# One recurrence step: the state kept once with four query products, the filtered attention turned for 6 and 10 sequences, the context's channels picked by products

## The chip, the cores and the metric

The kernel runs on one core of one Trainium2 chip. Its time is the device time of one execution in microseconds, and the number that counts is the median of several runs. The profile is one further execution, recorded with its instructions.

The engines are named as in the profile: PE is TensorE (PEld its loads of stationary operands, PE its matmuls), DVE is VectorE, ACT is ScalarE, POOL is GpSimd, SP is SyncE, which issues most DMAs here.

## The reference

The whole computation is two decoder layers for 16 sequences of 128 positions and 1024 channels. Layer 0 has a bidirectional state-space mixer, a cross-attention and a quantized feed-forward. Layer 1 has grouped-query attention, a recurrent attention decoder and a binarized feed-forward. A layer norm follows each. The change lies in the recurrent decoder of layer 1, which walks through the 128 positions one after the other:

```python
def step(carry, tgt):
    s, c, alpha = carry
    f = lax.conv_general_dilated(alpha, conv_w, (1,), 'SAME', dimension_numbers=('NCH', 'OIH', 'NCH'))
    e = jnp.einsum('a,bta->bt', va, jnp.tanh(enc_proj + (s @ Wa_s.T)[:, None, :] + jnp.einsum('bft,af->bta', f, Wa_f) + ba))
    e = jnp.where(mask, e, jnp.float32(-1e+30))
    alpha_new = jax.nn.softmax(e, axis=1)[:, None, :]
    g = jnp.einsum('bt,btd->bd', alpha_new[:, 0], hbatch)
    y = jnp.tanh(g @ L_gy_w.T + L_gy_b + s @ L_sy.T) @ L_yy_w.T + L_yy_b
    rec = tgt @ L_ys.T + s @ L_ss.T + g @ L_gs_w.T + L_gs_b
    ig, fg, cg, og = jnp.split(rec, 4, axis=1)
    c_next = _sig(fg) * c + _sig(ig) * jnp.tanh(cg)
    s_next = _sig(og) * jnp.tanh(c_next)
    return ((s_next, c_next, alpha_new), y)
```

Here s and c have 128 channels for each of the 16 sequences, alpha is the attention over the 128 positions of the memory, hbatch (the memory) has 256 channels, the filter has 10 channels of width 101, and rec has four gates of 128 channels. A position needs s, c and alpha of the position before it. The products with tgt and the outputs y do not sit inside the loop of the kernel: it keeps s and g of every position, and makes y from them afterwards.

## The kernel before

The stages follow each other: the mixer, the cross-attention, the feed-forward, the grouped-query attention, the recurrence (`decoder_scan`), and a last stage that makes the decoder's outputs and the final feed-forward (`stage_last`). While the attention's last group runs, `decoder_prepare` loads and prepares the constants of the recurrence on SP's queue (the products with tgt, scaled weights, filter bands). Everything is fp32 except where F32R or BF16 is named.

`decoder_scan` is a Python loop over the 128 positions, fully unrolled. `K.ordered` takes the order in which the loop issues its instructions and fixes it on PE, DVE, ACT, POOL and SP. So each engine runs its instructions in the order of the code, and waits come only from data and from buffers (PSUM tags such as `s1` and `s2` have one buffer each).

A position's step goes like this:

1. The PSUM tile `pf`, four banks of 512 columns (16 sequences of 32 memory positions in each), holds the argument of the tanh: the memory's projection, which ACT copies in (`pf<-enc`, L1128 and L1132), and on top of it, by products that accumulate (`onto`, L1056), the filtered attention (`waf` with `R`) and the state's query (`swr` with the 0/1 matrix `slot`).
2. `energies` (L1068, L1072): ACT takes the tanh of four sequences at a time into `th`, and PE multiplies it with `va`, which gives the energies.
3. Maximum, exponential, a transpose (L1122, L1152), and `aD`, in which each sequence's attention is a column of its own. The products of `aD` with the memory `hb` (L1149) give the context `pg`: 128 rows and 256 channels, where only row 32 * (b % 4) + b holds sequence b.
4. Sums and their reciprocals, and `gn`, the context divided by them (L1160, DVE). PE has meanwhile filtered the attention by products with banded matrices (L1164), and ACT scales the result into `fs` (L1169).
5. `gn` is turned so that channels lie on partitions: two transposes of 128 channels (L1175), each followed by a copy on DVE (L1176) that picks the 16 rows that hold sequences and writes them twice, for 32 columns of `gT`. POOL copies each half into the history (`ghist`, L1178).
6. The gates `gq`: own terms (L1081), the state's part (L1125: four column groups of 32, `sT` stationary) and the context's part (L1185: two halves of the channels times four groups). Then a tanh (L1188), two DVE operations to the new cell state (L1191, L1195), and the tanh `tc` of it (L1197).
7. `fs` is transposed into `ff` (L1199), and DVE turns the filtered attention of 8 sequences into `R` (L1201). A bf16 product that nobody reads (`keep_awake`) follows on PE, and the `waf` products for these 8 sequences (L1056).
8. The state `s` (L1206) is written four times side by side, 128 columns, and DVE transposes it in blocks of 32 (L1209): `sT` then holds the state four times, on 128 columns.
9. At the top of the next step, POOL copies the state into its history (L1092). One product with `sT` stationary gives the query `psw` on all 128 rows (L1099). DVE turns `R` for the other 8 sequences (L1100), splits the query into two F32R parts (`hi` L1102, `swr` L1104), and PE adds the `waf` products of the other 8 sequences and then the four `slot` products (L1056). With these, `pf` is complete and the next tanh can start.

Of the kernel before, what the change touches and what calls it, by code (L numbers as in the profile page):

```python
# [15 lines left out]
ALU = mybir.AluOpType  # L16
# [7 lines left out]
P = 128  # L24
NB = 16
# [880 lines left out]
LA_K = 101  # L906
LA_CHN = 10
LA_CH = 8


def decoder_prepare(K, keep, one, work, bank, pre, band, src):
# [5 lines left out]
    nc, a = K.nc, K.a  # L917
    D = {}
# [3 lines left out]
    D["gs"] = K.t(keep, [P, 2, 512], "gs")  # L922
    nc.sync.dma_start(D["gs"], a["la_gsT"].rearrange("(k p) n -> p k n", p=P))
    D["va"] = K.t(keep, [P, 63], "vaE")
    for n, k in (("ss", "la_ssT"), ("Was", "la_WasT"), ("waf", "la_Waf4"), ("dup", "k_dup")):
        D[n] = K.t(keep, [P, a[k].shape[1]], n)
        nc.sync.dma_start(D[n], a[k])

# [5 lines left out]
    for s in range(4):  # L934
        n = min(3, LA_CHN - 3 * s)
# [74 lines left out]
def decoder_scan(K, D, pre, ghist, shist, piece):  # L1010
# [5 lines left out]
    nc = K.nc  # L1016
    with ExitStack() as st:
        own = K.pool(st, "d_own")
        work = K.pool(st, "d_work", 2)
        ps = K.pool(st, "d_ps", 1, PSUM)  # L1020
# [4 lines left out]
        for k in range(4):  # L1025
            nc.tensor.matmul(pf[:, k].rearrange("p b t -> p (b t)"), zr[32 * k:32 * k + 32, :], D["slot"][32 * k:32 * k + 32, :],
                             start=True, stop=True, skip_group_check=True)
# [7 lines left out]
        aDb = bass.AP(aD.tensor, aD.offset, [aD.ap[0], [33, NB]])  # L1035
        pb = [K.t(own, [P, LA_CH, P], f"pb{i}") for i in range(2)]
        for t in pb:
# [1 line left out]

        z = K.t(work, [P, 5, 32], "z")  # L1040
        nc.vector.memset(z[:, 4], 0.0)
        sT = K.t(work, [P, P], "sT", bufs=4)
        nc.vector.memset(sT, 0.0)
        ff = K.t(ps, [P, 512], "ff")
        nc.vector.memset(ff, 1.0)

        taken = [bass.AP(ff.tensor, ff.offset + 8 * h, [ff.ap[0], [1, 8], [0, 2], [32, 16]]) for h in range(2)]
        def load_pre(ch):
            for q in range(4):
                nc.sync.dma_start(pb[ch % 2][32 * q:32 * q + 16, :, :],  # L1050
                                  pre[:, ch * LA_CH:(ch + 1) * LA_CH, q * P:(q + 1) * P])

        def onto(lhs, rhs, first, n):

            for k in range(4):
                nc.tensor.matmul(pf[:, k, first:first + n].rearrange("p b t -> p (b t)"), lhs[32 * k:32 * k + 32, :],  # L1056
                                 rhs[32 * k:32 * k + 32, 32 * first:32 * (first + n)], start=False, stop=True, skip_group_check=True)

        def keep_awake(n):

            for _ in range(n):
                idle = K.t(ps, [P, 512], "s2")
                nc.tensor.matmul(idle, D["identb"], D["wake"], start=True, stop=True)
# [16 lines left out]
        def own_terms(gq, l):  # L1080
            nc.tensor.matmul(gq, D["dup"], pb[(l // LA_CH) % 2][:, l % LA_CH, :], start=True, stop=False, skip_group_check=True)  # L1081

# [3 lines left out]
        R = None  # L1086
        traced = nc.cur_bb.bb.instructions
        for l in range(P):
            last = l + 1 == P
            if l % LA_CH == 0 and l + LA_CH < P:  # L1090
                load_pre(l // LA_CH + 1)
            nc.gpsimd.tensor_copy(shist[:, :, l], sT[:, 0:16])  # L1092
# [3 lines left out]
            if l:  # L1096

                psw = K.t(ps, [P, P], "s1")
                nc.tensor.matmul(psw, sT, D["Was"], start=True, stop=True)  # L1099
                nc.vector.transpose(R[:, 256:512].rearrange("p (b c) -> p b c", c=32), taken[1])  # L1100
                hi = K.t(work, [P, P], "hi", F32R)
                nc.vector.tensor_copy(hi, psw)  # L1102
                swr = K.t(work, [P, P], "swr", F32R)
                nc.vector.scalar_tensor_tensor(swr, hi.bitcast(F32), D["lohi"], psw, ALU.mult, ALU.add)  # L1104
                onto(D["waf"], R, 8, 8)
                onto(swr, D["slot"], 0, NB)

            pe = [K.t(ps, [P, P], "s1"), ff[:, 0:P]]
# [3 lines left out]
            gq = K.t(ps, [P, P], "gq")  # L1112
# [9 lines left out]
            nc.tensor.transpose(pT[0], ex[0], K.ident)  # L1122
            if l and not last:
                for q in range(4):
                    nc.tensor.matmul(gq[32 * q:32 * q + 32, :], sT[:, 0:32], D["ss"][:, q * P:(q + 1) * P], start=False, stop=False,  # L1125
                                     skip_group_check=True)
            if not last:
                nc.scalar.copy(pf[:, 0], D["enc"][:, 0])  # L1128
# [18 lines left out]
            for g in range(4):  # L1147
                for i in range(4):
                    nc.tensor.matmul(pg[32 * i:32 * i + 32, :], aD[:, 4 * g + i, :], D["hb"][:, 4 * g + i, :],  # L1149
                                     start=(g == 0), stop=(g == 3), skip_group_check=True)  # L1150
# [8 lines left out]
            gn = K.t(work, [P, 2, P], "gn")  # L1159
# [9 lines left out]
                nc.scalar.activation(fs.rearrange("p c t -> p (c t)"), ff[:, 0:3 * P], AF.Copy, scale=rx)  # L1169
                K.tc.add_manual_dep(traced[-1], copied.name, SYNC, reason="copies")  # L1170

            gT = K.t(work, [P, 2, 2, 16], "gT", bufs=4)
            for c in range(2):
                pgT = K.t(ps, [P, P], ("s2", "s1")[c])
                nc.tensor.transpose(pgT, gn[:, c], K.ident)  # L1175
                nc.vector.tensor_copy(gT[:, c].rearrange("p e (g i) -> p e g i", i=4),  # L1176
                                      bass.AP(pgT.tensor, pgT.offset, [pgT.ap[0], [0, 2], [4, 4], [33, 4]]))
                nc.gpsimd.tensor_copy(ghist[:, c, :, l], gT[:, c, 0, :])  # L1178
            if last:
                break  # L1180
            if l == 0:
                own_terms(gq, l)
            for c in range(2):
                for q in range(4):
                    nc.tensor.matmul(gq[32 * q:32 * q + 32, :], gT[:, c].rearrange("p e b -> p (e b)"),  # L1185
                                     D["gs"][:, c, q * P:(q + 1) * P], start=False, stop=(c == 1), skip_group_check=True)

            nc.scalar.activation(z[:, 0:4].rearrange("p g u -> p (g u)"), gq, AF.Tanh)  # L1188
# [4 lines left out]
            now, z = z, K.t(work, [P, 5, 32], "z")  # L1193
            C = z[:, 4]
            nc.vector.scalar_tensor_tensor(C, AB[:, 1], 0.5, AB[:, 0], ALU.mult, ALU.add)  # L1195
            tc = K.t(work, [P, 32], "tc")
            nc.scalar.activation(tc, C, AF.Tanh, scale=0.5)  # L1197
            for c in range(3):
                nc.tensor.transpose(ff[:, c * P:(c + 1) * P], fs[:, c, :], K.ident)  # L1199
            R = K.t(work, [P, 512], "R", bufs=1)  # L1200
            nc.vector.transpose(R[:, 0:256].rearrange("p (b c) -> p b c", c=32), taken[0])  # L1201
            keep_awake(1)
            onto(D["waf"], R, 0, 8)

            s = K.t(work, [P, 4, 32], "s")
            nc.vector.scalar_tensor_tensor(s, now[:, 2].unsqueeze(1).to_broadcast([P, 4, 32]), 1.0,  # L1206
                                           tc.unsqueeze(1).to_broadcast([P, 4, 32]), ALU.add, ALU.mult)
            sT = K.t(work, [P, P], "sT", bufs=4)
            nc.vector.transpose(sT, s.rearrange("p j u -> p (j u)"))  # L1209
        order()  # L1210


def stage_decoder(K, D, pre, src, out):
    with ExitStack() as st:
        hist = K.pool(st, "d_hist")
        ghist = K.t(hist, [P, 2, NB, P], "ghist")
        shist = K.t(hist, [P, NB, P], "shist")
        mkeep = K.pool(st, "m_keep")
        with ExitStack() as s2:
            W, piece = last_weights(K, mkeep, K.pool(s2, "m_raw"))  # L1220
            decoder_scan(K, D, pre, ghist, shist, piece)
        D["room"].close()
        stage_last(K, W, ghist, shist, src, out)
# [234 lines left out]
def rope_constants():  # L1458

    f = np.float32  # L1460
    theta, factor, hi, lo, L0 = 500000.0, 32.0, 4.0, 1.0, 2048
    idx = np.arange(0, 32, 2, dtype=f) / f(32)
    freq = f(1.0 / (2.0 * np.pi)) * np.power(f(theta), -idx)
    scaled = np.where(freq < f(lo / L0), freq / f(factor), freq)
    smooth = np.clip((f(L0) * freq - f(lo)) / f(hi - lo), f(0), f(1))
    mid = (f(1) - smooth) * (freq / f(factor)) + smooth * freq
    freq = np.where((freq >= f(lo / L0)) & (freq <= f(hi / L0)), mid, scaled).astype(f)
    phase = f(2.0 * np.pi) * np.arange(P, dtype=f)[:, None] * freq[None, :]
    emb = np.concatenate([phase, phase], -1)

    sign = np.where(np.arange(32) % 32 < 16, -1.0, 1.0).astype(f)
    return [np.ascontiguousarray(np.tile(t.astype(f).T, (4, 1))) for t in (np.cos(emb), np.sin(emb) * sign)]


def shape_constants():
    f = np.float32
    o = {}
    r = np.arange(P)

    step, seq = r // 8, r % 8  # L1480
    same = seq[:, None] == seq[None, :]
    o["k_seq_masks"] = np.stack([same & (step[:, None] < step[None, :]), same & (step[:, None] > step[None, :])], 1).astype(f)
    o["k_step_masks"] = np.stack([step[:, None] < np.arange(16)[None, :], step[:, None] > np.arange(16)[None, :]], 1).astype(f)
    o["k_cos"], o["k_sin"] = rope_constants()
    o["k_causal"] = np.where(r[:, None] >= r[None, :], 0.0, -1e30).astype(f)

    o["k_slot"] = (r[:, None] % 16 == np.arange(512)[None, :] // 32).astype(f)

    o["k_half"] = np.stack([1.0 - (r % 32 // 8 == 1), (r % 32 // 8 == 1)], 1).astype(f)
    o["k_lohi"] = np.where(r % 32 < 16, 0.0, -1.0).astype(f).reshape(P, 1)  # L1490

    n = np.arange(64)
    n = np.arange(16)

    o["k_dup"] = (r[:, None] == (r - r % 32 + r % 16)[None, :]).astype(f)

    o["k_quad"] = (r[:, None] % 32 == np.arange(8)[None, :]).astype(f)
    o["k_time"] = np.tile(np.arange(P, dtype=f), (P, 1))
    return o


def layout(i):
# [61 lines left out]
    o["mo_gT"] = c(i[p + "gate_w"].T)  # L1564
    o["mo_b"], o["mo_in"], o["mo_out"] = (c(i[p + n]) for n in ("bias", "in_channel_scale", "out_channel_scale"))
    o.update(shape_constants())
    return o

# [13 lines left out]
```

## Time and profile before

| what | value |
|---|---|
| median of 3 runs | 3615.65 us (3613.06 to 3617.14) |
| profiled execution, its own time | 3607.57 us |
| span of the profiled execution | 3605.8 us |
| granted PE clock, mean over the span | 0.948 |
| recurrence | from about 1890 us to about 3290 us |
| one step, gn to gn | 10.96 us |
| PE / DVE / ACT / POOL busy | 88% / 51% / 38% / 27% |

A row of the profile names the line, the engine, the operation, what it writes and reads, the shape, and the count. For PE, `128*32` means a tile of 128 rows and 32 columns of the array. Each record of a matmul is one pass: fp32 products have two records each, transposes one. The ends of matmuls are modelled, so two groups on PE can seem to overlap a little. PSUM tiles of the same tag share a name, so `s` in these rows stands for `psw`, `pgT`, `pg` and `pe`.

### The profile page before, as it was taken

The page shows a single profiled execution, that of the slowest core. Times are in us where ns is not written, and L with a number is a line of the kernel's source. Part 1 is how long each engine was busy: PE and PEld are TensorE (multiplying, and loading weights), DVE is VectorE, ACT ScalarE, POOL GpSimd, SP SyncE. Part 2 cuts the span into 40 slices and gives each one's busy share as a digit, 9 for nine tenths or more (in the row PEclk, how much of TensorE's full clock was granted, in tenths as well). Part 3 has the DMA queues.
Part 4 walks back from the last instruction along what each step waited for, and adds up shares of the span by engine and source line. Part 5 has one row for each costly group of instructions (what it writes and reads, how often), then busy time and mean ns, then how long its engine had stood idle before and what let it go on. Part 6 is the DMA issues. An engine that isn't in the chain of part 4 may idle for free.

```text
span 3605.8 us, 60750 instructions
## 1 busy us (share of the span) xinstructions
PE 3168.9 (88%) x24202; PEld 1696.6 (47%) x24202; DVE 1852.8 (51%) x5044; ACT 1378.1 (38%) x3521; POOL 978.3 (27%) x1106
## 2 busy tenths in 40 slices
PE   7778886888899999999998888888888888887998
PEld 3444453666454555455544444444444444443455
DVE  5785775666244545453334444444444444444665
ACT  4433332111032333232225555555555555553211
POOL 3334763455233233331110111111111111112453
PEclk8778998999989999998999999999999999998898
DMA  5001222111410101022211000000000000001111
GB/s 184 1 1 47 98 78 93 47 59 47 148 36 12 47 24 47 24 81 69 87 40 41 5 11 11 5 11 5 10 5 10 5 10 5 5 2 48 35 59 47
DMA packets 72213, 144.12 MB, mean 40 GB/s; under 512 B 10042, under 2 KB 34490, under 8 KB 71930
## 3 DMA queue, kind: packets, MB, share of 16 engines
q1 hardware_dynamic: 65562, 122.74, 10.3%
q10 hardware_dynamic: 6368, 17.50, 1.2%
q8 instruction: 191, 3.13, 0.4%
q14 instruction: 92, 0.75, 0.1%
HBM read 102.47 MB, written 39.06 MB: 39 GB/s over the span
## 4 chain that ended last, share of the span: by engine, by line
PE 53%; DVE 9%; ACT 9%; issue 2%; POOL 1%; DMA 0%; POOLq 0%; DVEq 0%; ACTq 0%; SPq 0%
PE p L784 8%; ACT th L1068 7%; PE s L1149 7%; PE p L855 6%; PE pf L1056 4%; PE p L1002 3%; PE m L1386 3%; PE gq L1185 2%; PE ff L1164 2%; PE t L833 2%; PE s L812 2%; PE p L797 2%; PE ff L1072 2%; PE s L1099 2%; DVE R L1201 1%
## 5 line engine op out<-in xcount | busy, mean ns | idle before, releaser
L1068 ACT ACTIVATE th<-pf 128x512 f32<-128x512 f32 x512 | 264.4, 602 | 331.1 <-PE pf L1056 331.0
L1178 POOL COPY ghist<-gT 128x16 f32<-128x16 f32 x256 | 44.8, 214 | 979.5 <-DVE gT L1176 979.5
L821 ACT ACTIVATE s<-s,nm 128x128 f32<-128x128 f32 x512 | 198.2, 389 | 253.1 <-DVE nm L818 220.4
L1149 PE MATMUL s<-hb,aD 128*32 128x256 f32 x4096 | 275.5, 387 | 0.6 <-DVE aD L1138 0.6
L1056 PE MATMUL pf<-R,waf 32*128 32x256 f32 x2032 | 181.4, 426 | 69.6 <-DVE R L1201 69.6
L855 PE MATMUL p<-ga_Wo,cT 128*128 128x512 f32 x512 | 228.7, 595 | 0.0
L1132 ACT COPY pf<-enc 128x512 f32<-128x512 f32 x381 | 224.8, 590 | 8.1
L784 PE MATMUL p<-xT,ga_Wq 128*128 128x512 f32 x512 | 226.4, 597 | 0.0
L824 POOL TENSOR_TENSOR s<-s,rs 128x512 f32<-128x512 f32 x128 | 133.3, 1041 | 321.6 <-DVE rs L823 314.8
L1077 DVE TENSOR_REDUCE nm<-s 128x1 f32<-128x128 f32 x128 | 37.4, 292 | 288.2 <-PE s L1072 288.2
L91 POOL TENSOR_TENSOR ln_rs<-ln_ve,neghalf 128x1 f32<-128x1 f32 x96 | 55.6, 582 | 380.8 <-DVE ln_ve L89 363.9
L784 PEld LDWEIGHTS p<-xT,ga_Wq 128*128 128x128 f32 x512 | 95.4, 190 | 113.8 <-issue 111.0
L855 PEld LDWEIGHTS p<-ga_Wo,cT 128*128 128x128 f32 x512 | 93.8, 190 | 113.8 <-issue 111.7
L1149 PEld LDWEIGHTS s<-hb,aD 128*32 128x32 f32 x4096 | 106.5, 109 | 84.2 <-DVE aD L1138 46.1
L1056 PEld LDWEIGHTS pf<-R,waf 32*128 32x128 f32 x2032 | 79.3, 182 | 134.1 <-DVE R L1201 118.8
L1072 PE MATMUL s<-th,vaE 128*32 128x128 f32 x2048 | 109.3, 286 | 36.4 <-ACT th L1068 28.5
L1169 ACT ACTIVATE fs<-ff,rx 128x384 f32<-128x384 f32 x127 | 73.8, 581 | 172.4 <-DVE rx L1167 169.1
L835 DVE COPY pT<-t 128x512 f32<-128x512 f32 x128 | 88.0, 687 | 87.6 <-PE t L833 87.3
L1072 PE MATMUL ff<-th,vaE 128*32 128x128 f32 x2048 | 109.3, 286 | 16.2
L1002 PE MATMUL p<-xT,qT 128*128 128x512 f32 x256 | 115.2, 603 | 0.0
L856 DVE TENSOR_TENSOR xr<-p,xr 128x512 f32<-128x512 f32 x32 | 22.1, 692 | 168.5 <-PE p L855 168.5
L812 PE MATMUL s<-kT,qT 32*128 32x128 f32 x1024 | 108.0, 315 | 0.0
(342 smaller groups left out, 6878.4 us busy)
## 6 DMA issues: line engine op xcount, KB each, us to landing
x<-x SPq DMA_DIRECT2D x95, 512.0 KB
xt<-xT SPq DMA_DIRECT2D x8, 1024.0 KB
x<-x ACTq DMA_DIRECT2D x16, 512.0 KB
xr<-x SPq DMA_DIRECT2D x16, 512.0 KB
x<-xr SPq DMA_DIRECT2D x16, 512.0 KB
out<-x ACTq DMA_DIRECT2D x16, 512.0 KB
ga_Wq<-ga_Wq SPq DMA_DIRECT2D x2, 2048.0 KB
ga_Wo<-ga_Wo SPq DMA_DIRECT2D x2, 2048.0 KB
```

The costliest lines, as they stand in the source:

```text
L784: nc.tensor.matmul(pq, lhsT, xT[:, k].rearrange("p i t -> p (i t)"), start=(k == 0), stop=(k == 7))
L812: nc.tensor.matmul(psc[n][:, r, :], qT[sl, 4 * kc + r, i, :], kT[sl, kc, i, :], start=True, stop=True)
L821: nc.scalar.activation(s[:, r, :], s[:, r, :], AF.Exp, bias=nm[:, r:r + 1], accum_out=sm[:, r:r + 1])
L824: nc.gpsimd.tensor_tensor(s, s, rs.unsqueeze(2).to_broadcast([P, 4, P]), ALU.mult)
L855: nc.tensor.matmul(po, cT[:, k, :], w["o"][h][:, k, :], start=(k == 0), stop=(k == 7))
L1002: nc.tensor.matmul(py, xT[:, k, b % 4, :], ys[:, k, :], start=(k == 0), stop=(k == 7))
L1056: nc.tensor.matmul(pf[:, k, first:first + n].rearrange("p b t -> p (b t)"), lhs[32 * k:32 * k + 32, :], rhs[32 * k:32 * k + 32, 32 * first ...
L1068: nc.scalar.activation(th.rearrange("p i (k t) -> p i k t", t=32), pf[:, :, 4 * g:4 * g + 4, :].rearrange("p k i t -> p i k t"), AF.Tanh)
L1072: nc.tensor.matmul(pe[32 * i:32 * i + 32, :], D["va"][:, 31 - b:63 - b], th[:, i, :], start=False, stop=(g % 2 == 1), skip_group_check=True)
L1132: nc.scalar.copy(pf[:, k], D["enc"][:, k])
L1149: nc.tensor.matmul(pg[32 * i:32 * i + 32, :], aD[:, 4 * g + i, :], D["hb"][:, 4 * g + i, :], start=(g == 0), stop=(g == 3), skip_group_che ...
L1386: nc.tensor.matmul(pm[:, h, :], xp[:, k, :], w[:, k, h * 512:(h + 1) * 512], start=(k + n == 0), stop=(k + n == 8))
```

## The change

The change has three parts, all in the recurrence.

The context's channels: the two transposes and the two copies are replaced. A new constant `pick` (128 rows, 32 columns, 0 or 1) has a one in column j at row 32 * (b % 4) + b with b = j % 16. Each half of `gn` is now the stationary operand of an fp32 product with `pick`, which puts the picked 16 sequences, twice, straight into 32 columns of one PSUM tile. One copy of 64 columns moves both halves to `gT`, and one POOL copy writes the history. `decoder_prepare` loads `pick` with one DMA more.

The state: `s` and `sT` have 32 columns instead of 128. The query is made by four products, each of which writes 32 rows of `psw` with the same 32 columns of `sT` stationary.

The filtered attention: `R` is turned for 6 sequences first and for 10 in the next step, where it was 8 and 8, and the `waf` products are split alike.

```diff
+LA_ONE = 6
 ...
-    for n, k in (("ss", "la_ssT"), ("Was", "la_WasT"), ("waf", "la_Waf4"), ("dup", "k_dup")):
+    for n, k in (("ss", "la_ssT"), ("Was", "la_WasT"), ("waf", "la_Waf4"), ("dup", "k_dup"),
+                 ("pick", "k_pick")):
         D[n] = K.t(keep, [P, a[k].shape[1]], n)
         nc.sync.dma_start(D[n], a[k])
 ...
-        sT = K.t(work, [P, P], "sT", bufs=4)
+        sT = K.t(work, [P, 32], "sT", bufs=4)
         nc.vector.memset(sT, 0.0)
 ...
-        taken = [bass.AP(ff.tensor, ff.offset + 8 * h, [ff.ap[0], [1, 8], [0, 2], [32, 16]]) for h in range(2)]
+        taken = [bass.AP(ff.tensor, ff.offset + first, [ff.ap[0], [1, n], [0, 2], [32, 16]])
+                 for first, n in ((0, LA_ONE), (LA_ONE, NB - LA_ONE))]
 ...
                 psw = K.t(ps, [P, P], "s1")
-                nc.tensor.matmul(psw, sT, D["Was"], start=True, stop=True)
-                nc.vector.transpose(R[:, 256:512].rearrange("p (b c) -> p b c", c=32), taken[1])
+                for k in range(4):
+                    nc.tensor.matmul(psw[32 * k:32 * k + 32, :], sT, D["Was"], start=True, stop=True)
+                nc.vector.transpose(R[:, 32 * LA_ONE:].rearrange("p (b c) -> p b c", c=32), taken[1])
 ...
-                onto(D["waf"], R, 8, 8)
+                onto(D["waf"], R, LA_ONE, NB - LA_ONE)
                 onto(swr, D["slot"], 0, NB)
 ...
-            gT = K.t(work, [P, 2, 2, 16], "gT", bufs=4)
+            pgT = K.t(ps, [P, 2, 32], "s2")
             for c in range(2):
-                pgT = K.t(ps, [P, P], ("s2", "s1")[c])
-                nc.tensor.transpose(pgT, gn[:, c], K.ident)
-                nc.vector.tensor_copy(gT[:, c].rearrange("p e (g i) -> p e g i", i=4),
-                                      bass.AP(pgT.tensor, pgT.offset, [pgT.ap[0], [0, 2], [4, 4], [33, 4]]))
-                nc.gpsimd.tensor_copy(ghist[:, c, :, l], gT[:, c, 0, :])
+                nc.tensor.matmul(pgT[:, c], gn[:, c], D["pick"], start=True, stop=True)
+            gT = K.t(work, [P, 2, 32], "gT", bufs=4)
+            nc.vector.tensor_copy(gT, pgT)
+            nc.gpsimd.tensor_copy(ghist[:, :, :, l], gT[:, :, 0:16])
 ...
             R = K.t(work, [P, 512], "R", bufs=1)
-            nc.vector.transpose(R[:, 0:256].rearrange("p (b c) -> p b c", c=32), taken[0])
+            nc.vector.transpose(R[:, 0:32 * LA_ONE].rearrange("p (b c) -> p b c", c=32), taken[0])
             keep_awake(1)
-            onto(D["waf"], R, 0, 8)
-
-            s = K.t(work, [P, 4, 32], "s")
-            nc.vector.scalar_tensor_tensor(s, now[:, 2].unsqueeze(1).to_broadcast([P, 4, 32]), 1.0,
-                                           tc.unsqueeze(1).to_broadcast([P, 4, 32]), ALU.add, ALU.mult)
-            sT = K.t(work, [P, P], "sT", bufs=4)
-            nc.vector.transpose(sT, s.rearrange("p j u -> p (j u)"))
+            onto(D["waf"], R, 0, LA_ONE)
+            s = K.t(work, [P, 32], "s")
+            nc.vector.scalar_tensor_tensor(s, now[:, 2], 1.0, tc, ALU.add, ALU.mult)
+            sT = K.t(work, [P, 32], "sT", bufs=4)
+            nc.vector.transpose(sT, s)
 ...
+    b = np.arange(32) % 16
+    o["k_pick"] = (r[:, None] == (32 * (b % 4) + b)[None, :]).astype(f)
```

More of the change, by code (lines that the diff above doesn't have):

```diff
@@ L1124, in decoder_scan @@
                 for q in range(4):
-                    nc.tensor.matmul(gq[32 * q:32 * q + 32, :], sT[:, 0:32], D["ss"][:, q * P:(q + 1) * P], start=False, stop=False,
+                    nc.tensor.matmul(gq[32 * q:32 * q + 32, :], sT, D["ss"][:, q * P:(q + 1) * P], start=False, stop=False,
                                      skip_group_check=True)
@@ L1184, in decoder_scan @@
                 for q in range(4):
-                    nc.tensor.matmul(gq[32 * q:32 * q + 32, :], gT[:, c].rearrange("p e b -> p (e b)"),
+                    nc.tensor.matmul(gq[32 * q:32 * q + 32, :], gT[:, c],
                                      D["gs"][:, c, q * P:(q + 1) * P], start=False, stop=(c == 1), skip_group_check=True)
@@ L1490, in shape_constants @@
     o["k_lohi"] = np.where(r % 32 < 16, 0.0, -1.0).astype(f).reshape(P, 1)
-    n = np.arange(64)
-    n = np.arange(16)
+    b = np.arange(32) % 16
+    o["k_pick"] = (r[:, None] == (32 * (b % 4) + b)[None, :]).astype(f)
     o["k_dup"] = (r[:, None] == (r - r % 32 + r % 16)[None, :]).astype(f)
```

## The prediction

> **What bounds the kernel.** The page first: the span, the engines, the chain.
>
> ```profile
> span 3605.8 us, 60750 instructions
> PE 3168.9 (88%) x24202; PEld 1696.6 (47%) x24202; DVE 1852.8 (51%) x5044; ACT 1378.1 (38%) x3521; POOL 978.3 (27%) x1106
> ...
> PE 53%; DVE 9%; ACT 9%; issue 2%; POOL 1%; DMA 0%; POOLq 0%; DVEq 0%; ACTq 0%; SPq 0%
> ```
>
> No engine bounds it alone: DMA has nothing in the chain, and the chain changes engines. The edits lie in the recurrence, so its stage decides. Busy time by windows (columns: window, length, PE, PEld, DVE, ACT, POOL busy, granted clock, DMA share, GB/s):
>
> ```profile
> 2350.00:2800.00 450.00, 399.15 (x5340) 188.34 (x5336) 204.46 (x863) 243.49 (x533) 49.49 (x157) 1.00 0.03 8
> ...
> 3388.00:3402.00 14.00, 13.86 (x26) 6.91 (x27) 8.40 (x10) 2.06 (x2) 2.35 (x1) 0.52 0.00 0
> ```
>
> The clock stands at full speed in the recurrence, no engine is full, and POOL and DMA are nearly idle. The stage is a serial loop, and a step is as long as its chain. Its tail, from the timeline of one step (start, busy us, engine, line, operation, what ended the wait):
>
> ```profile
> 2412.51 0.48 DVE L1160 TENSOR_SCALAR gn<-s,rs 128x256 f32<-128x256 f32 x1 [0.44 <-PE s L1149]
> 2413.05 0.44 PE L1175 MATMUL s<-ident,gn 128*128 128x128 f32 x2
> 2413.41 0.30 DVE L1176 COPY gT<-s 128x32 f32<-128x32 f32 x2
> 2413.66 0.64 PE L1185 MATMUL gq<-gs,gT 128*32 128x128 f32 x16 [0.17 <-DVE gT L1176]
> 2414.37 0.28 ACT L1188 ACTIVATE z<-gq 128x128 f32<-128x128 f32 x1 [0.37 <-PE gq L1185]
> 2414.94 0.19 DVE L1195 SCALAR_TENSOR_TENSOR z<-AB 128x32 f32<-128x32 f32 x1
> 2415.05 0.44 DVE L1201 STREAM_TRANSPOSE R<-ff 128x256 f32<-128x256 f32 x1
> 2415.16 0.23 ACT L1197 ACTIVATE tc<-z 128x32 f32<-128x32 f32 x1 [0.52 <-DVE z L1195]
> 2415.42 0.29 DVE L1206 SCALAR_TENSOR_TENSOR s<-z,tc 128x128 f32<-128x128 f32 x1
> 2415.54 0.71 PE L1056 MATMUL pf<-R,waf 32*128 32x256 f32 x8 [0.55 <-DVE R L1201]
> 2415.75 0.31 DVE L1209 STREAM_TRANSPOSE sT<-s 128x128 f32<-128x128 f32 x1
> 2415.99 0.41 DVE L1100 STREAM_TRANSPOSE R<-ff 128x256 f32<-128x256 f32 x1
> 2416.19 0.30 PEld L1099 LDWEIGHTS s<-Was,sT 128*128 128x128 f32 x2 [0.33 <-issue]
> 2416.61 0.71 PE L1056 MATMUL pf<-R,waf 32*128 32x256 f32 x8
> 2416.71 0.29 DVE L1102 CAST hi<-s 128x128 fp32r<-128x128 f32 x1 [0.32 <-PE s L1099]
> 2417.44 0.19 PEld L1056 LDWEIGHTS pf<-slot,swr 32*128 32x128 f32 x4 [0.52 <-DVE swr L1104]
> ```
>
> Normalised context gn, turn, copy, gate products, gates, state s, its transpose, query product, hi, swr, slot products; then the next tanh. The line for gn stood at 2401.55 one step earlier: 10.96 us a step, 127 times, 1392 of 3605.8 us. So 0.057 us a step is 7.2 us, 0.2% of the time, about what a measurement of this kernel can tell from no change.
>
> **The picked channels (on the chain).** Removed: two transposes (two PE records) and two 32-column copies, where the gate products started after the first copy. Added: two fp32 products with 32 columns and one 64-column copy. A product of this kind, 128 loaded columns and few streamed ones, stands in the last stage:
>
> ```profile
> 3450.22 0.97 PEld L1337 LDWEIGHTS t<-sel,lg 128*128 128x128 f32 x8 [1.57 <-ACT lg L1334]
> 3450.22 1.06 PE L1337 MATMUL t<-sel,lg 128*128 128x8 f32 x8 [0.74 <-ACT lg L1334]
> ```
>
> Those are four products: two loads and two passes each. A load lasts 0.19, so they follow each other every (0.97 - 0.19) / 7 = 0.111 us, and two products (four records) take 1.06 - 4 x 0.111 = 0.61. Streaming 32 columns, not 8, adds 0.02 (L1149 with 256 columns takes 0.64 for 8 records, L1125 with 128 takes 0.43: 0.21 per 128 columns in two passes). From the first load at 2413.04: products done 2413.67, copy from 2413.71 (hi starts 0.03 after L1099's modelled end). The copy costs 0.192 (L1176, 32 columns) plus 0.034 for 32 more (L1191 0.225 at 64 columns against L1195 0.192 at 32): done 2413.94. Gate products start 0.05 later as now, at 2413.99 instead of 2413.66: **+0.335**. They take 0.64 as before, since their second channel already waited for PE only. The transposes of fs (L1199) follow them on PE, so they move too, and still end before R needs them. One ghist copy on POOL in place of two is off the chain.
>
> Here the Trainium skill says otherwise ("TensorE: Matmul & The Clock Gate", LDWEIGHTS): a load costs its columns over 1.2 GHz, 107 ns for 128, whatever is loaded. Then the edit is two more loads, 0.21, plus 0.034 for the copy: +0.25, which the gain below cancels (+1 us in all). The trace shows the transposes' two loads done within 0.20 us, so 0.06 apart, and product loads 0.111 apart: the removed loads were the cheap kind. I take the rows.
>
> **State once, four query products, 6 and 10 (on the chain).** The state operation shrinks from 128 to 32 columns: 0.293 to 0.192 (L1195). Its transpose is not shown at 32 columns: from L1209 (0.311 at 128) and L1100 (0.406 at 256) 0.74 ns a column, 0.24; by L1191 and L1195's 1.04 ns, 0.21. I take 0.21: sT ready 0.20 earlier. It is not what the query product waits for, though. sT ends at 2416.06, the load comes 0.13 later, where DVE to PE otherwise takes 0.05 (R ends 2415.49, L1056 starts 2415.54). The load starts 0.06 before the modelled end of L1056 (2416.25), as the next L1056 starts 0.07 before L1099's (2416.68), and as L1199 starts 0.07 before L1185's, with fs ready 0.24 earlier: PE changing the shape of its tiles. So PE must come free, and the split decides. R for 6 sequences: 64 columns less, 0.067 at 1.04 ns (0.05 at 0.74). L1056 with 192 columns: 0.107 less by the 0.21 per 128. PE free 0.174 earlier (0.157): I take **-0.17**; with sT the later one it would be nearly the same. The four query products in column groups are L1125's shape exactly, 0.43 for 8 records, against 0.49 from load to end now: **-0.06**. hi, swr and the slot products keep their size. Shortening R does not bring s forward: s starts 0.03 after tc, and still does.
>
> The cover of what moves: the second R (10 sequences, 0.47) ends at about 2416.26, before hi at 2416.48. The second L1056, 0.82, runs from about 2416.37 to 2417.19, and the slot products want PE at 2417.20. That is 0.01 of margin by modelled ends (0.1 more if a group of the same shape starts before them); beyond it each 0.1 is 0.1 lost.
>
> The pick constant is one more 16 KB load on SP, once: SP's L927 loads issue in about 0.5 us. Behind it stand the filter bands and the preparation's loads, where PE waits in turn on attention work: 0, at most 1 us.
>
> **The sum.** +0.335 - 0.17 - 0.06 = +0.10 us a step, times 127 = **+12.6 us** on the profiled execution: its own time was 3607.57, 1.8 around the span, so 3620. The median of the runs shown, 3615.65, lies 8.1 above that execution. Carried over: **3628**. With the ends of the unknowns (transpose, R, copy: loss 0.30 to 0.36, gain 0.22 to 0.30) net 0 to +0.14 a step: 3616 to 3634.
>
> **Rivals.**
> *Same.* The shape change costs PE nothing between 32-row and 32-column tiles. Then only sT decides: gain 0.20 + 0.06 and up to 0.04 more, net +0.04, +5 us: 3621. For it: the trace has no such pair; against: all neighbouring pairs show the gap.
> *Faster.* The picked products run in one pass, as the transposes of the same gn do. Loads 0.06 apart, done at about 2413.35, gate products at 2413.66: loss 0.01, net -0.22, 127 x -0.22 = -28 us: 3587. It decides as soon as the edit costs under 0.18. Against it: every fp32 product on the page has two records each.
> *Slower, by the clock.* PE streams less in the tail: the two products stream 32 columns where the transposes streamed 128, and a wait grows by 0.33. At 1890 to 1897 the first step runs at half clock, and L1149's 24 records take 2.52 instead of 1.50: about 2 us for such a step. One step in ten makes +26 on top: 3654. For it: at 3388 the clock was 0.52 with PE busy, so busy time is no safeguard. Against it: 1400 us at 1.00 now, whatever the phase. The skill's same page (Part 4) says that transposes do not count as activity for the gate: by that the edit adds counted streaming and the clock stays; by busy time it risks this. I keep 1.00 as likeliest.
> That the query products do not run side by side (0.6 more a step) L1125 speaks against.
>
> **Chances.** The sum 0.62 (own range 3623 to 3636: its ends and the spread of the runs), clock 0.12, same 0.18, faster 0.08. Slower by over 0.2%: 0.74. The range 3614 to 3645 leaves out the faster case, most of the clock's and the edge of the same.
>
> **What would show it.** Gate products start about 1.0 us after gn ends (0.67 now); the picked products have 4 records, loads 0.11 apart; s to query load shrinks from 0.77 to 0.60; slot load minus s start from 2.02 to 1.79; step 11.06; clock 1.00. It is wrong if the picks have 2 records, if the slot products wait for L1056 instead of swr, or if half-clock stretches appear between 1900 and 3300.

## The result, and the profile after

The changed kernel is slower. Over 19 runs of each its median is 3623.15 us (3617.99 to 3635.07), that of the kernel before 3614.54 (3608.36 to 3617.14). The ratio is 1.0032, with a 95% interval of 1.0024 to 1.0040: 0.3%, or about 12 us (8.7 to 14.5). In a second series it was 1.0046 (1.0030 to 1.0063). The profiled execution took 3622.88 us, with a span of 3621.1.

The page of the changed kernel first:

```profile
span 3621.1 us, 62404 instructions
PE 3181.1 (88%) x25220; PEld 1719.5 (47%) x25220; DVE 1825.9 (50%) x4916; ACT 1377.9 (38%) x3521; POOL 964.0 (27%) x978
...
PE 53%; DVE 9%; ACT 9%; issue 3%; POOL 1%; DMA 1%; POOLq 0%; DVEq 0%; SPq 0%; ACTq 0%
```

PE has 1018 matmul records more, DVE 128 instructions fewer and 27 us less to do, POOL 128 fewer. None of them was full, so none of these sums decides anything. The same stretch of the recurrence as before, by windows:

```profile
2350.00:2800.00 450.00, 399.51 (x5603) 193.59 (x5595) 193.29 (x815) 240.97 (x528) 42.38 (x111) 1.00 0.03 8
```

The clock is granted in full, as before. The time is in the steps. From gn to gn a step takes 11.089 us (the median of its 127 distances) where it took 10.958, so 0.131 us more, and 127 times that is 16.6 us. The timeline of the changed kernel, at the places shown of before:

```profile
2408.55 0.48 DVE L1165 TENSOR_SCALAR gn<-s,rs 128x256 f32<-128x256 f32 x1 [0.51 <-PE s L1154]
2409.09 0.52 PEld L1179 LDWEIGHTS s<-pick,gn 128*128 128x128 f32 x4 [0.66 <-DVE gn L1165]
2409.09 0.63 PE L1179 MATMUL s<-pick,gn 128*128 128x32 f32 x4
2409.76 0.23 DVE L1181 COPY gT<-s 128x64 f32<-128x64 f32 x1 [0.39 <-PE s L1179]
2410.03 0.38 PEld L1189 LDWEIGHTS gq<-gs,gT 128*32 128x32 f32 x16 [0.43 <-DVE gT L1181]
2410.61 0.55 PE L1203 MATMUL ff<-ident,fs 128*128 128x128 f32 x3
2410.75 0.28 ACT L1192 ACTIVATE z<-gq 128x128 f32<-128x128 f32 x1 [0.71 <-PE gq L1189]
2410.89 0.10 PEld L1067 LDWEIGHTS <-identb 128*128 128x128 bf16 x1
2410.99 0.38 PE L1067 MATMUL s<-wake,identb 128*128 128x512 bf16 x1
2411.43 0.37 DVE L1205 STREAM_TRANSPOSE R<-ff 128x192 f32<-128x192 f32 x1
2411.80 0.19 DVE L1209 SCALAR_TENSOR_TENSOR s<-z,tc 128x32 f32<-128x32 f32 x1
2411.86 0.61 PE L1060 MATMUL pf<-R,waf 32*128 32x192 f32 x8 [0.48 <-DVE R L1205]
2412.03 0.21 DVE L1211 STREAM_TRANSPOSE sT<-s 128x32 f32<-128x32 f32 x1
2412.39 0.43 PE L1104 MATMUL s<-Was,sT 128*32 128x128 f32 x8
2412.75 0.82 PE L1060 MATMUL pf<-R,waf 32*128 32x320 f32 x8
2412.89 0.29 DVE L1107 CAST hi<-s 128x128 fp32r<-128x128 f32 x1 [0.24 <-PE s L1104]
2413.61 0.19 PEld L1060 LDWEIGHTS pf<-slot,swr 32*128 32x128 f32 x4 [0.55 <-DVE swr L1109]
```

Two distances carry the story. From the end of gn (2409.03) to the gate products' first load (2410.03) is 1.00 us, and was 0.67. From the start of s (2411.80) to the slot products' load (2413.61) is 1.81, and was 2.02. Over steps 20 to 99 the medians are 1.002 against 0.666, and 1.809 against 2.017: one part lost 0.336 us, the other won 0.208. All else in the step stands where it stood.

### The profile page after: what moved, and what is told of

Its sections match the earlier page's. It is cut to its first block, busy times and chain, and to the rows that moved or that the text cites. A ratio compares the mean times of both kernels' runs of the same rounds, so it can differ in the third digit from the quotient of the medians.

```text
span 3621.1 us, 62404 instructions
## 1 busy us (share of the span) xinstructions
PE 3181.1 (88%) x25220; PEld 1719.5 (47%) x25220; DVE 1825.9 (50%) x4916; ACT 1377.9 (38%) x3521; POOL 964.0 (27%) x978
## 4 chain that ended last, share of the span: by engine, by line
PE 53%; DVE 9%; ACT 9%; issue 3%; POOL 1%; DMA 1%; POOLq 0%; DVEq 0%; SPq 0%; ACTq 0%
PE p L784 8%; ACT th L1072 7%; PE s L1154 7%; PE p L855 6%; PE pf L1060 4%; PE p L1004 3%; PE m L1388 3%; PE gq L1189 2%; PE ff L1169 2%; PE s L1179 2%; PE t L833 2%; PE s L812 2%; PE p L797 2%; PE ff L1076 2%; PE s L1104 1%
## 5 line engine op out<-in xcount | busy, mean ns | idle before, releaser
L1182 POOL COPY ghist<-gT 128x32 f32<-128x32 f32 x128 | 31.2, 244 | 1021.4 <-DVE gT L1181 1021.4
L1060 PE MATMUL pf<-R,waf 32*128 32x192 f32 x2032 | 181.4, 426 | 61.3 <-DVE R L1205 61.3
L1189 PE MATMUL gq<-gs,gT 128*32 128x128 f32 x2032 | 81.8, 279 | 39.9 <-DVE gT L1181 39.9
L675 PE MATMUL acc<-w_up,qt 128*128 128x512 f32 x256 | 76.9, 450 | 38.2 <-DVE qt L613 34.8
```

Of the source, the lines that this page charges most:

```text
L1189: nc.tensor.matmul(gq[32 * q:32 * q + 32, :], gT[:, c], D["gs"][:, c, q * P:(q + 1) * P], start=False, stop=(c == 1), skip_group_check=True)
```

## The experiments

### Each part alone

The first run puts only the picked channels into the kernel before. The second takes only them out of the changed kernel.

```diff
 pick_alone, against the kernel before
-            gT = K.t(work, [P, 2, 2, 16], "gT", bufs=4)
             for c in range(2):
-                nc.tensor.transpose(pgT, gn[:, c], K.ident)
-                nc.vector.tensor_copy(gT[:, c]..., pgT...)
+                nc.tensor.matmul(pgT[:, c], gn[:, c], D["pick"], start=True, stop=True)
+            nc.vector.tensor_copy(gT, pgT)
 ... (with the load of pick, the tiles and POOL's copy, as in the whole change)
 state_split, against the changed kernel: the same lines the other way round
```

> The kernel before, with the picked channels alone (two fp32 products with pick, one copy of 64 columns). My theory: this part costs the step 0.336 us, as the changed kernel shows from the end of gn to the gate products' first load (1.002 against 0.666), and nothing else moves: a step of 11.294 us, 127 x 0.336 = 43 us more than before, ratio about 1.012. Rival (the part costs little, and the rest of the change was neutral): a step of about 11.09 and 17 us more.

> The changed kernel with the two transposes and the two copies of the channels put back: the state once, four query products, and 6 and 10 sequences. My theory: this part saves 0.207 us a step, so 10.751 us, 127 x 0.207 = 26 us less than before, ratio about 0.993. Rival (the rest of the change is neutral, the picks cost 0.13): a step of 10.96 and the time of before. The stages outside the recurrence should take what they take in before; if the load of pick moved them, the part of the time outside the steps returns to that of before.

pick_alone has a step of 11.300 us, and its ratio is 1.0122 (1.0095 to 1.0149); its median is 3658.86 us beside 3614.78. state_split has a step of 10.751 us, and its ratio is 0.9937 (0.9918 to 0.9956), 3590.4 beside 3614.78. So the picks cost 0.342 us a step, the rest saves 0.207, and the sum, 0.135, is the 0.131 of the changed kernel. The change is one edit that wins some 26 us and one that loses some 43. The rival, a neutral rest and a cheap pick, is out.

### Where the picks lose

pick_two_copies lets the first half of the channels go ahead. pick_f32r makes each product a single pass; it rounds the context, so it is a probe and not a replacement. Each has one execution, so their steps are compared and not their times. The steps repeat well: the changed kernel's took 11.089 us in two profiles, and load_alone, which has the steps of before, 10.966 beside 10.958.

```diff
 pick_two_copies, against the changed kernel
-            pgT = K.t(ps, [P, 2, 32], "s2")
+            gT = K.t(work, [P, 2, 32], "gT", bufs=4)
             for c in range(2):
-                nc.tensor.matmul(pgT[:, c], gn[:, c], D["pick"], start=True, stop=True)
+                pgT = K.t(ps, [P, 32], ("s2", "s1")[c])
+                nc.tensor.matmul(pgT, gn[:, c], D["pick"], start=True, stop=True)
+                nc.vector.tensor_copy(gT[:, c], pgT)
 ... (POOL's copy by halves too)
 pick_f32r, against the changed kernel
-            gn = K.t(work, [P, 2, P], "gn")
+            gn = K.t(work, [P, 2, P], "gn", F32R)
-                nc.tensor.matmul(pgT[:, c], gn[:, c], D["pick"], start=True, stop=True)
+                nc.tensor.matmul(pgT[:, c], gn[:, c], D["pickr"], start=True, stop=True)
 ... (pickr is pick, copied once into F32R)
```

> The changed kernel, with each half of the channels in a PSUM tile of its own and copied by itself (32 columns), so that the first half's gate products can start before the second half's product. My theory (0.22 of the loss is that the gate products wait for all four loads, 0.03 the longer copy): first half's load 0.22 earlier, gate products end where the second half allows: second copy ends 0.93 after gn, its products start 0.98 and take 0.43, so z starts 0.25 earlier than in the changed kernel, a step of 10.84. Rival (the loads themselves hold PE, whatever is copied when): a step within 0.05 of 11.089.

> The changed kernel with gn and pick in F32R, so that each picked product is one pass (2 PE records in place of 4); the context is rounded to F32R on its way to the gates and the history. My theory (the loss is the two more loads at 0.11 each, plus the copy): products done 0.22 earlier, a step of 10.87. Rival (what costs is the product's latency and the single copy, not the second pass): 11.05 to 11.09.

pick_two_copies has a step of 10.833 us, 0.256 less than the changed kernel. Its timeline:

```profile
2408.87 0.48 DVE L1165 TENSOR_SCALAR gn<-s,rs 128x256 f32<-128x256 f32 x1 [0.15 <-PE s L1154]
2409.41 0.52 PEld L1180 LDWEIGHTS s<-pick,gn 128*128 128x128 f32 x4 [0.66 <-DVE gn L1165]
2409.86 0.42 DVE L1181 COPY gT<-s 128x32 f32<-128x32 f32 x2 [0.17 <-PE s L1180]
2410.11 0.65 PE L1189 MATMUL gq<-gs,gT 128*32 128x128 f32 x16
```

PE's loads are as long as before (0.52 for four). But the gate products start 0.75 us after gn ends in place of 1.00, because the first half's copy starts before the second half's product is done. The loss left against state_split, where that distance is 0.67, is 0.082 us a step. So about three quarters of the loss go away when the first half need wait neither for the second half's product nor for the wider copy (0.225 us for 64 columns, where 32 take 0.19), and one quarter stays.

pick_f32r has a step of 10.853 us:

```profile
2404.43 0.30 PEld L1181 LDWEIGHTS s<-pickr,gn 128*128 128x128 f32 x2 [0.66 <-DVE gn L1167]
2404.43 0.40 PE L1181 MATMUL s<-pickr,gn 128*128 128x32 f32 x2
2404.86 0.23 DVE L1183 COPY gT<-s 128x64 f32<-128x64 f32 x1 [0.16 <-PE s L1181]
2405.14 0.38 PEld L1191 LDWEIGHTS gq<-gs,gT 128*32 128x32 f32 x16 [0.41 <-DVE gT L1183]
```

Two loads in place of four, still 0.11 apart (0.30 for two of 0.19), and the products end 0.236 us earlier; the step is 0.236 shorter. This is what the second passes of the two fp32 products cost. The savings of the two runs (0.256 and 0.236) must not be added: they are two views of the same 0.22 us. It is gone if the passes are not made, and also if the first half need not wait for the second half's passes.

### What the query product waits for

The prediction held that the narrower state would bring nothing by itself, because the query product waits for PE to leave the waf products, and that the split frees PE. Each of the two was done alone, and the split was taken one further.

```diff
 state_8_8, against state_split
-LA_ONE = 6
+LA_ONE = 8
 split_alone, against the kernel before
-taken = [... ff.offset + 8 * h, [ff.ap[0], [1, 8], ...] for h in range(2)]
+taken = [... ff.offset + first, [ff.ap[0], [1, n], ...] for first, n in ((0, 6), (6, 10))]
 ... (R and onto split alike)
 state_5_11, against state_split
-LA_ONE = 6
+LA_ONE = 5
```

> The kernel before with the state once and the four query products, but still 8 and 8 sequences, and with the old transposes. It tells what the query product waits for. My theory (PE must first end the waf products of the 8 sequences and change its tile shape): sT is ready 0.20 earlier, but the query's load still starts 0.76 after s starts, and only the product is 0.03 shorter: a step of 10.92. Rival (the load waits for sT): load 0.17 to 0.20 earlier, a step of 10.73 to 10.76, as with 6 and 10.

> The kernel before with 6 and 10 sequences alone: four copies of the state and one query product stay. My theory (with PE free earlier the query waits for sT, which ends 0.13 before the load now): sT to load falls from 0.125 to between 0.05 and 0.12, a step of 10.88 to 10.95. Rival (PE alone sets it): 0.17 less, a step of 10.78.

> As state_split (old transposes, state once, four products), with 5 and 11 sequences. My theory: PE is free 0.087 earlier (0.033 from R, 0.053 from the products), then sT is the later one; the load moves by 0.03 to 0.09, the second waf products still end before the slot products: a step of 10.66 to 10.72, ratio to before about 0.991. Rival (the second waf products, now for 11, hold up the slot products): a step of 10.75 or more.

| kernel | step, us | s start to query load | sT end to query load | against before, us a step |
|---|---|---|---|---|
| before | 10.958 | 0.763 | 0.125 | |
| state_8_8 | 10.923 | 0.761 | 0.322 | -0.035 |
| split_alone | 10.949 | 0.754 | 0.116 | -0.009 |
| state_split (6 and 10) | 10.751 | 0.588 | 0.150 | -0.207 |
| state_5_11 | 10.733 | 0.554 | 0.116 | -0.225 |

The narrow state alone wins 0.035 us, and both together 0.207. The split alone shows 0.009, which is no more than the 0.008 between before and load_alone, whose steps are the same. In the timeline of state_8_8:

```profile
2403.07 0.71 PE L1059 MATMUL pf<-R,waf 32*128 32x256 f32 x8 [0.55 <-DVE R L1205]
2403.18 0.21 DVE L1211 STREAM_TRANSPOSE sT<-s 128x32 f32<-128x32 f32 x1
2403.71 0.16 PEld L1103 LDWEIGHTS s<-Was,sT 128*32 128x32 f32 x8 [0.33 <-issue]
```

sT is done at 2403.39, and the load stands until 2403.71, 0.07 before the modelled end of the waf products (2403.78). "issue" in the bracket means that no semaphore shows what PE waited for. In split_alone PE is free, and the other reason appears:

```profile
2408.74 0.61 PE L1059 MATMUL pf<-R,waf 32*128 32x192 f32 x8 [0.48 <-DVE R L1204]
2409.01 0.31 DVE L1212 STREAM_TRANSPOSE sT<-s 128x128 f32<-128x128 f32 x1
2409.44 0.30 PEld L1102 LDWEIGHTS s<-Was,sT 128*128 128x128 f32 x2 [0.39 <-PE pf L1059]
```

The waf products end at 2409.35, and the load comes at 2409.44, after sT (2409.32), at the same 0.116 after sT's end as in state_5_11. So the kernel before had two bounds within 0.01 us of each other, and neither edit could bring the load forward without the other. The bracket names the waf products, but they ended 0.09 before the load, and where PE's last group sets the start, this load comes 0.07 before its end (0.072 in before, state_8_8 and state_split). What is left is sT.

In state_5_11 the load meets that bound too:

```profile
2404.70 0.55 PE L1059 MATMUL pf<-R,waf 32*128 32x160 f32 x8 [0.45 <-DVE R L1205]
2404.91 0.21 DVE L1211 STREAM_TRANSPOSE sT<-s 128x32 f32<-128x32 f32 x1
2405.23 0.19 PEld L1103 LDWEIGHTS s<-Was,sT 128*32 128x32 f32 x8 [0.22 <-issue]
```

It has a ratio of 0.9935 (0.9914 to 0.9957), 3588.16 us beside 3613.99. Its step lies just above the 10.66 to 10.72 that were expected: the load comes 0.034 earlier than in state_split, but hi follows it 0.513 later in place of 0.494, and why is open. Its step is at the 0.116 that sT allows, so a still smaller first part should have nothing more to give here. Its 0.018 us a step below state_split are about 2 us, too little for a comparison of times to tell. Both beat the kernel before and the changed one.

The 0.116 belongs to these kernels. In all that keep the transposes PE runs a semaphore instruction of 0.051 us between sT and this load (`EVENT_SEMAPHORE` at L1099 in before, at L1103 in state_5_11). The changed kernel has none there, and in it the loads that wait for a DVE result with PE free, those for pick, the gates and slot, start 0.053 us after it. So with the picks a smaller first part might still win something; no run tried it.

### The load, the clock, and the rest of the time

The steps account for 16.6 us, and the first ratio for about 12, with an interval that ends at 14.5. load_alone asks whether the load of pick makes the difference outside the steps; after_again repeats the changed kernel; after_no_wake, one execution, asks how near the clock came to falling.

```diff
 load_alone, against the kernel before
-    for n, k in (..., ("dup", "k_dup")):
+    for n, k in (..., ("dup", "k_dup"), ("pick", "k_pick")):
 after_no_wake, against the changed kernel
-            keep_awake(1)
 after_again: the changed kernel as it is
```

> The kernel before with the load of pick alone, which nobody reads. It tells whether this load moves the time outside the steps, where the changed kernel's runs show some 5 us less than its steps account for. My theory (it doesn't; the spread comes from the clock outside the recurrence): a step of 10.958 and a ratio of 1.000 within 0.002. Rival (the load shifts the preparation's other loads and saves 5 us): ratio about 0.9985.

> The changed kernel once more, for a second profile and more runs beside the kernel before. In the first profile the steps account for 127 x 0.131 = 16.6 us, the ratio 1.0032 for 11.6. My theory (the steps always take the same, the rest is spread from the clock outside the recurrence): a step of 11.089 again, time outside the steps anywhere from 2210 to 2230, and a ratio between 1.003 and 1.006. Rival (the change saves some 5 us outside the steps): ratio at most 1.0035 again, and time outside the steps below that of before.

> The changed kernel without the idle bf16 product that follows the transposes of fs on PE (nobody reads it). It asks how near the clock rival was[...]. My theory (the clock has room to spare in the recurrence): granted clock 1.00 between 1900 and 3300, a step of 11.09. Rival (the thin tail is close to the gate's limit): half-clock stretches in the recurrence, steps up to 2 us longer, hundreds of us in all.

load_alone: a step of 10.966 us and a ratio of 0.9997 (0.9985 to 1.0010). The load costs nothing that can be measured, and saves nothing. after_again: a step of 11.089 us again, and a ratio of 1.0046 (1.0030 to 1.0063), which is 16.6 us. So the steps are the same in both series, and the 5 us that the first one lacks did not come back in the second: there the runs spend 2217.0 us outside the steps in the mean (the span of each run less the steps of the profile), and those of before beside them 2217.4. What made the 5 us in the first series stays open; the load of pick is ruled out. The time outside the steps (span less the stretch from the first gn to the last) lies between 2208.8 and 2228.2 us in the twelve profiles and goes (correlation 0.97) with the time that the clock record shows at half speed: 2208.8 at 359 us of half clock (split_alone), 2212.7 at 370 (the changed kernel), 2214.1 at 376 (before), 2228.2 at 410 (pick_f32r). With two exceptions, both in after_no_wake, none of the half-clock stretches starts between the first gn and the last.

after_no_wake has a step of 11.092 us but for two. Windows of it around 2160:

```profile
2150.00:2160.00 10.00, 8.55 (x129) 4.23 (x121) 3.96 (x19) 5.93 (x13) 0.24 (x1) 1.00 0.11 30
2160.00:2164.00 4.00, 4.00 (x44) 1.97 (x41) 1.11 (x4) 1.27 (x3) 0.21 (x1) 0.57 0.00 0
2164.00:2194.00 30.00, 25.93 (x379) 12.78 (x375) 13.16 (x57) 16.53 (x37) 3.54 (x8) 1.00 0.01 2
2194.00:2198.00 4.00, 4.00 (x48) 1.98 (x41) 1.11 (x4) 1.30 (x3) 0.22 (x1) 0.57 0.00 0
```

Without the idle product the clock falls twice in the recurrence, for 3.4 us each time, and the two steps that it meets take 11.82 and 11.78 us. Neither expectation is met: there is no wide room, and no collapse. This is one profile beside two of the changed kernel without a fall, so that the product holds the clock up is likely and not shown beyond doubt.

## Why the prediction was right, and where it was off

**What bounds the kernel.** Right: every edit was worth what it did to the serial chain, and the 27 us less of DVE work were worth nothing.

**The picked channels.** Predicted +0.335 us, measured 0.336 in the changed kernel and 0.342 alone. The row in the last stage that it was taken from (L1337) gave it term by term: loads 0.11 apart, products 0.63, a copy of 0.225. The rule of the Trainium skill ("TensorE: Matmul & The Clock Gate", LDWEIGHTS), which prices a load by its columns alone, gives an estimate of 0.25. Its 0.107 us for 128 columns agrees with the fp32 products' loads, 0.111 apart; the transposes' loads, also of 128 columns, come 0.06 apart, and that it leaves out. That the gate products had started on the first half alone was in the sum, as a difference of start times; the runs show it to be most of the loss.

**The state and the split.** Predicted -0.23 us (0.17 and 0.06), measured -0.207. The first term, the earlier query load, was 0.175 by start of s (0.763 to 0.588), as worked out, and for the reason given: state_8_8 shows PE as the bound, split_alone shows sT right behind it. The second term, the query product itself, was mis-sized. The four query products do take 0.43, but hi starts 0.067 after their modelled end, where it started 0.037 after that of the single product (medians; in the steps shown 2412.82 and 2412.89, before 2416.68 and 2416.71). The semaphore events of the trace tell which side is late: the product's own event comes 0.472 us after its first load, 0.504 before the change, and hi starts 0.023 after that event in both. So the modelled end of the four lies 0.03 too early against that of the one, and the gain was 0.03, not 0.06. The profile of before had a row that shows this: z starts 0.07 after the gate products, which also are column groups. sT took 0.211 at 32 columns, the value chosen.

**The cover.** The second waf products end 0.04 before the slot products' load, which still waits for swr; the margin given was 0.01 to 0.11. It held.

**The sum.** +0.10 us a step and +12.6 us were forecast (the rounded terms give 0.105 and 13.3), and the steps show +0.131 and +16.6. The difference is nearly all the term above. That the measured ratio, about 12 us, hits the forecast is in part luck: it is the 16.6 less the 5 us outside the steps, which were not forecast and which the second series does not show.

**The rivals.** One pass a product: the trace shows two, and pick_f32r shows that they are what the case hung on. A free shape change between 32-row and 32-column tiles: state_8_8 speaks against it, the load stands 0.07 before the modelled end, as between the other neighbours of 32-row, 32-column and full tiles. One pair that changes shape shows no such gap: with tiles of 32 and then 16 columns, the load (L1164 behind L1149 in before) comes 0.40 before the end. Groups of one shape follow closer too: the idle product's load (L1067, 2410.89 in the changed kernel) comes 0.27 before the modelled end of the transposes of fs (L1203, 2411.16). The clock: it stayed at 1.00 in both profiles of the changed kernel, but in after_no_wake, with one product of 512 columns less in a step (0.38 us by its row), it fell twice. Whether transposes count for the clock, on which the skill (Part 4 of the same page) and the busy time differ, no run here has settled: after_no_wake took away a product, not a transpose. Two falls that cost 0.7 us each are also much cheaper than the 2 us taken from the first step; the stretch of 3.4 us covers only part of a step of 11.09.

## What to carry to other kernels

When two operations are merged into one, ask who was waiting for the first of them alone: here one copy in place of two made the chain 0.256 us longer, as the first half could have been on its way while the second was being made. Price a replaced PE instruction by a row of its own kind (transposes one cheap pass, fp32 products two), not by its shape. And where two bounds end together, test the edits as a pair: alone they were worth 0.035 and 0.009 us, together 0.207.

## What the runs showed of the hardware

The modelled end of a column-group product lies further ahead of its real one than that of a full-width product: the product's semaphore event came 0.044 us after it for the query and the gate products of the changed kernel, 0.014 for its picked products and for the single query product of before, and the next engine started 0.023 after the event each time (in state_5_11 it was 0.033 for the query products). A query load behind DVE's transpose came 0.116 us after its end in both kernels where nothing else held it, with a semaphore instruction of 0.051 us on PE before it; loads without one came 0.053 after other DVE results. And with a product that nobody reads, 0.38 us long by its row, the clock of the recurrence stood at full speed in both profiles of the changed kernel, and without it, in the one profile taken, it fell twice.
